# Issuing every cosine table load from ScalarE's queue in a transformer block kernel

## The chip, the cores and the metric

The kernel runs on one core of one Trainium2 chip. The metric is the device time in microseconds (us); the time before is the median of three runs. A profile of one further execution gives each engine's instructions. Engines are named as the profile names them: PE (TensorE matmuls), PEld (its weight loads), DVE (VectorE), ACT (ScalarE), POOL (GpSimd), SP (SyncE, which here only issues DMAs). A trailing q, as in SPq or ACTq, marks what an engine's sequencer does, such as issuing a DMA or waiting for a semaphore.

## What is computed

One transformer block on 2048 tokens of width 1024, all in float32:

```
h = layernorm(x)
q, k, v = h @ Wq, h @ Wk, h @ Wv           # 16 heads of 64
q, k = rotary(q), rotary(k)                # t * cos + swap_pairs(t) * sin
a = softmax(causal(q k^T) / 8) v
x = x + layernorm(a @ Wo)
f = (silu(h2 @ Wg^T) * (h2 @ Wu^T)) @ Wd^T  # h2 = layernorm(x); weights are 4-bit codes times scales
out = x + layernorm(f)
```

The change concerns the rotary step: the tables of cosines and sines, by position and feature, lie in HBM (`cos_sin`, 128 x 2 x 2048) and are loaded in pieces of 512 positions.

## The kernel before

Float32 products are made as three reduced-precision ones: each operand is split into a high part (a cast on ACT, L120) and the rest (a subtraction on DVE, L121), and `mm3` (L112 to L114) issues three matmuls. The work goes through these stages.

- **Ramp**, about 0 to 190 us. `make_x` normalizes the rows, transposes and splits them; `prep_w` loads the q, k and v weights of a feature block m of 128 columns (`wf`, L179) and splits them (L186 on ACT, L190 or L194 for the rest). `both` then calls `qkv(m, c, ..., ramp=True)` for m = 0 and 1 and the four position blocks c: eight groups.
- **Attention**, about 190 to 1320 us. For pair = 0 to 6, two heads are attended (`scores` from L262, `weighted` from L313), and beside them, between their matmuls, run the groups `qkv(m, c)` of the blocks m = 2 to 7: 24 groups that call `qkv` without `ramp`. Each of these loads its transposed rows again (`xc`, L222, four loads). For the first group of a block the three `wf` loads come ahead. The last pair's attention reaches to about 1480 us.
- **Output projection** and second layer norm, to about 1660 us, then the feed-forward part with its code lookup, to the end.

One group `qkv(m, c)` runs as follows. It takes a slot for the table `tab` and loads 512 KB into it (L232). For q and then k: 24 matmuls into a PSUM bank, a copy to `t1` by ACT (L251), a shuffle by DVE (L253), the product with the cosines by DVE (L254), that with the sines by POOL (L255), their sum by POOL (L256), a split into `hl`, and a store of 512 KB to `qs` or `ks` in HBM (L259). For v: a copy, four transposes, a split into `vo` and a store to `vs` (L249). The heads of block m read `q`, `k` and `v` back from there (L342, L335, L336).

`tab`, `vo`, both `hl` and the three `wf` all take their place from one set of four slots of 8 KB per partition, tagged "f4". A slot is free for a new tile when all that reads the old one is done: for `hl` and `vo` that is the landing of their store.

Nearly all DMAs are issued by SP, in the order of its own instruction list (`load = nc.sync.dma_start`). The only exception before is the eight table loads of the ramp, which ACT issues. An engine's instruction list, ACT's with its DMA issues included, is worked through in order; an instruction that must wait holds back all behind it.

No order is written out by hand, except a few "pace" edges that tie some matmuls of a group to matmuls of the attention. The program is built with `tile.TileContext(nc, schedule_with_timeline_sim=True)`: a planner runs the program on its own model of durations, and the order in which instructions go out there becomes the fixed order of each engine. The semaphore waits keep the result right when the chip's durations differ from the planned ones. So a change in one instruction's queue can shift the order of others behind it in all engines' lists.

Of the kernel before, what the change touches and what calls it, by code (L numbers as in the profile page):

```python
# [57 lines left out]
def block_kernel(ctx, tc, x, wq, wk, wv, wo, gu_codes, gu_scales, d_codes, d_scales, cos_sin, out):  # L58
    nc = tc.nc
    V, A, G, T = nc.vector, nc.scalar, nc.gpsimd, nc.tensor  # L60
    load = nc.sync.dma_start
# [12 lines left out]
    def slot(tag, shape, dtype, name):  # L74
        assert int(np.prod(shape[1:])) * 4 <= SLOTS[tag][1] * 1024, (tag, shape)
        return sb.tile(shape, dtype, tag=tag, name=name, bufs=SLOTS[tag][0])

    def bank(tag, name="bk"):
        return ps.tile([P, 512], F32, tag=tag, name=name, bufs=BANKS[tag])
# [22 lines left out]
    def f32(ap):  # L102
        return ap.bitcast(F32)
# [6 lines left out]
    def mm3(o, w, xx, first, last):  # L110

        r = T.matmul(o, lhsT=w[:, 0], rhs=xx[:, 0], start=first, stop=False)  # L112
        T.matmul(o, lhsT=w[:, 0], rhs=xx[:, 1], start=False, stop=False)  # L113
        T.matmul(o, lhsT=w[:, 1], rhs=xx[:, 0], start=False, stop=last)  # L114
        return r
# [3 lines left out]
    def split(hi, lo, src):  # L119
        high[:] = [A.copy(hi, src)]  # L120
        return V.tensor_tensor(lo, src, f32(hi), ALU.subtract)  # L121
# [107 lines left out]
    def qkv(m, c, ws, xs, ramp=False, pace=None):  # L229
        cs = slice(c * 512, (c + 1) * 512)  # L230
        tab = slot("f4", [P, 2, 512], F32, "tab")
        (A.dma_start if ramp else load)(tab, cos_sin[:, :, cs])  # L232
        for n, w in enumerate(ws):
            o = bank("S" if ramp and n != 1 else "F", "qkv")
            for k in range(KE):
                mm = mm3(o, w[k], xs[k // 2][:, :, k % 2, :], k == 0, k == KE - 1)
                if k == 0 and pace:
                    pace(mm, n)
            t1 = slot("t2", [P, 512], F32, "t1")
            if n == 2:  # L240
                A.copy(t1, o)
                pv = bank("F", "pv").rearrange("p (t n) -> p t n", t=4)
                for t in range(4):
                    T.transpose(pv[:, t, :], t1[:, t * P : (t + 1) * P], ident)
                vo = slot("f4", [P, 4, 2, 2, D], FR, "vo")
                src = pv.rearrange("p t (a d) -> p t a d", a=2)
                for a in range(2):
                    split(vo[:, :, a, 0, :], vo[:, :, a, 1, :], src[:, :, a, :])
                load(vs[m][cs].rearrange("(t p) a n -> p t (a n)", p=P), f32(vo.rearrange("p t a l d -> p t (a l d)")))  # L249
            else:  # L250
                A.copy(t1, o)  # L251
                sh = slot("t2", [P, 512], F32, "sh")
                V.stream_shuffle(sh, t1, [i ^ 1 for i in range(32)])  # L253
                V.tensor_tensor(t1, t1, tab[:, 0, :], ALU.mult)  # L254
                G.tensor_tensor(sh, sh, tab[:, 1, :], ALU.mult)  # L255
                G.tensor_tensor(t1, t1, sh, ALU.add)  # L256
                hl = slot("f4", [P, 2, 512], FR, "hl")
                split(hl[:, 0, :], hl[:, 1, :], t1)
                load((qs, ks)[n][m][:, :, cs], f32(hl))  # L259
# [96 lines left out]
    def both(*steps):  # L356
        for m, c in steps:
            qkv(m, c, first[m], xs[c], ramp=True)
# [25 lines left out]
    def group(m, c, xs=None, pace=None):  # L384
        if m not in ws:
            ws[m] = prep_qkv(m)
        qkv(m, c, ws[m], xs or load_x(c), pace=pace)

    for pair in range(KE - 1):
# [27 lines left out]
        for i, (m, c) in enumerate(now):  # L417

            def pace(mm, n):
                want = PACE * (3 * i + n) / (3 * len(now)) * anchors[-1][0]  # L420
                after(mm, next(a for a in anchors if a[0] >= want)[1])
# [418 lines left out]
```

## Time and profile before

| what | value |
|---|---|
| median of three runs | 3014.03 us (3012.47 to 3019.24) |
| profiled execution, its time | 3014.01 us |
| profiled execution, span of its instructions | 3012.1 us |
| busy: PE, DVE, ACT, POOL | 97%, 68%, 56%, 32% of the span |
| mean granted TensorE clock | 0.991 |
| DMA queue q1 (issued by SP) | 529.10 MB |
| DMA queue q10 (issued by ACT) | 4.19 MB, 2176 packets |
| `tab` loads | 24 from SP, 8 from ACT, 512 KB each |

The page of a profile lists busy time by engine, then the span in 40 equal slices (about 75 us each) with the busy tenths of each engine. A group row names the line, the engine, the operation and its tiles as out<-in, then the busy time and the idle time before it with what ended it. A wait row reads "who <- whom: us in total, times, longest". A timeline row gives start, duration, engine, line and, in brackets, the idle time just before and what ended it.

### The profile page before, as it was taken

How to read it: one execution, taken by the hardware profiler on the slowest of the kernel's cores; microseconds unless marked ns; L12 is line 12 of the kernel's file. 1: busy time of each engine (PE TensorE's matmuls, PEld its weight loads, DVE VectorE, ACT ScalarE, POOL GpSimd, SP SyncE). 2: the span in 40 equal slices, each digit the busy share in tenths (PEclk: the TensorE clock that was granted, in tenths of full speed). 3: DMA queues.
4: the chain of work that ended last, by engine and by line, in shares of the span. 5: the costliest groups of instructions: out<-in, count | busy, mean ns of one | idle time of the engine just before them, and what ended most of it. 6: DMA issues, size and time to landing. Idle time of an engine off the chain costs nothing.

```text
span 3012.1 us, 42532 instructions
## 1 busy us (share of the span) xinstructions
PE 2917.0 (97%) x14168; PEld 2409.7 (80%) x14168; DVE 2035.8 (68%) x4171; ACT 1698.4 (56%) x3569; POOL 953.0 (32%) x1055
## 2 busy tenths in 40 slices
PE   7989999999998999999999999999999999999998
PEld 6868888787887787777788788888888887888887
DVE  6567778886777778777665767776666677444347
ACT  4256667776666667667555655655555566333234
POOL 4344344443434343445322121222211223100034
PEclk9999999999999999999999999999999999999999
DMA  8787665757556468463456444444334444744446
GB/s 287 277 249 233 214 222 177 222 161 220 172 195 182 146 202 260 137 210 105 123 187 213 130 134 143 151 133 140 131 119 140 138 153 146 254 141 148 150 144 234
DMA packets 271740, 536.01 MB, mean 178 GB/s; under 512 B 22944, under 2 KB 113056, under 8 KB 255648
## 3 DMA queue, kind: packets, MB, share of 16 engines
q1 hardware_dynamic: 269344, 529.10, 54.6%
q10 hardware_dynamic: 2176, 4.19, 0.4%
q8 instruction: 112, 1.84, 0.3%
q14 instruction: 108, 0.88, 0.1%
HBM read 371.98 MB, written 161.22 MB: 177 GB/s over the span
## 4 chain that ended last, share of the span: by engine, by line
PE 79%; DMA 10%; DVE 4%; ACT 2%; POOL 2%; issue 1%; SPq 1%; POOLq 0%; ACTq 0%; DVEq 0%
PE bk L112 14%; PE bk L114 14%; PE bk L113 14%; PE pt L320 6%; PE qkv L112 4%; PE qkv L113 4%; PE qkv L114 4%; PE o L325 3%; PE o L324 3%; PE s L278 3%; PE s L280 3%; DMA wf<-in_wq 3%; PE pj L469 2%; PE pj L471 2%; PE pj L470 2%
## 5 line engine op out<-in xcount | busy, mean ns | idle before, releaser
L310 POOL TENSOR_SCALAR prob<-prob,rc 128x512 f32<-128x512 f32 (+3 forms) x640 | 405.4, 659 | 436.4 <-DVE rc L305 219.6
L112 PE MATMUL bk<-x,wt 128*128 128x512 f32 x1376 | 534.0, 390 | 2.7 <-ACT wt L120 1.8
L113 PE MATMUL bk<-x,wt 128*128 128x512 f32 x1376 | 535.2, 389 | 0.0
L114 PE MATMUL bk<-x,wt 128*128 128x512 f32 x1376 | 535.1, 389 | 0.0
L288 ACT ACTIVATE prob<-s,mxs 128x512 f32<-128x512 f32 (+3 forms) x640 | 402.6, 632 | 147.8 <-DVE mxs L286 90.6
L121 DVE TENSOR_TENSOR pw<-pt,pw 128x512 fp32r<-128x512 f32 (+3 forms) x640 | 378.4, 602 | 119.7 <-ACT pw L120 118.0
L534 ACT ACTIVATE ln<-cs,bias 128x512 f32<-128x512 f32 x520 | 360.0, 716 | 109.2 <-DVE m L541 25.4
L120 ACT CAST pw<-pt 128x512 fp32r<-128x512 f32 (+3 forms) x640 | 324.1, 527 | 171.6 <-PE pt L320 140.6
L320 PE MATMUL pt<-ident,prob 128*128 128x128 f32 x2176 | 345.5, 275 | 6.8 <-DVE pw L121 5.5
L320 PEld LDWEIGHTS pt<-ident,prob 128*128 128x128 f32 x2176 | 267.6, 141 | 61.7 <-issue 7.2
L112 PEld LDWEIGHTS bk<-x,wt 128*128 128x128 f32 x1376 | 258.2, 188 | 57.5 <-ACT wt L120 2.6
L286 DVE TENSOR_REDUCE mxs<-s 128x1 f32<-128x512 f32 x384 | 260.9, 681 | 60.0 <-PE s L280 59.1
L114 PEld LDWEIGHTS bk<-x,wt 128*128 128x128 f32 x1376 | 258.3, 188 | 53.8
L113 PEld LDWEIGHTS bk<-x,wt 128*128 128x128 f32 x1376 | 258.3, 188 | 53.5
L278 PE MATMUL s<-k,q 128*128 128x512 f32 (+3 forms) x640 | 265.7, 416 | 25.1 <-ACT prob L288 22.4
L325 PE MATMUL o<-pw,v 128*128 128x512 f32 (+3 forms) x640 | 247.3, 388 | 9.5 <-DVE pw L121 9.0
L324 PE MATMUL o<-pw,v 128*128 128x512 f32 (+3 forms) x640 | 244.3, 382 | 9.8 <-ACT pw L120 7.9
L112 PE MATMUL qkv<-xc,w 128*128 128x512 f32 x576 | 231.8, 402 | 10.3 <-ACT w L186 6.3
L113 PE MATMUL bk<-bt,at 128*128 128x512 f32 x616 | 239.6, 389 | 0.0
L114 PE MATMUL bk<-bt,at 128*128 128x512 f32 x616 | 238.8, 389 | 0.0
L112 PE MATMUL bk<-bt,at 128*128 128x512 f32 x616 | 238.7, 389 | 0.0
L280 PE MATMUL s<-k,q 128*128 128x512 f32 (+3 forms) x640 | 236.6, 372 | 0.0
(150 smaller groups left out, 5513.8 us busy)
## 6 DMA issues: line engine op xcount, KB each, us to landing
xc<-xd SPq DMA_DIRECT2D x96, 1024.0 KB, 9.3
q<-qs SPq DMA_DIRECT2D x128, 256.0 KB, 7.2
ast<-S SPq DMA_DIRECT2D x44, 512.0 KB, 3.9
cs<-in_gu_scales SPq DMA_DIRECT2D x172, 128.0 KB, 3.2
cs<-in_gu_codes SPq DMA_DIRECT2D x86, 256.0 KB, 3.0
A<-in SPq DMA_DIRECT2D x66, 256.0 KB, 2.0
S<-in SPq DMA_DIRECT2D x66, 256.0 KB, 3.2
ast<-A SPq DMA_DIRECT2D x33, 512.0 KB, 4.5
```

Of the source, the lines that this page charges most:

```text
L112: r = T.matmul(o, lhsT=w[:, 0], rhs=xx[:, 0], start=first, stop=False)
L113: T.matmul(o, lhsT=w[:, 0], rhs=xx[:, 1], start=False, stop=False)
L114: T.matmul(o, lhsT=w[:, 1], rhs=xx[:, 0], start=False, stop=last)
L121: return V.tensor_tensor(lo, src, f32(hi), ALU.subtract)
L278: mm = T.matmul(s, lhsT=q[:, 0, j * P : (j + 1) * P], rhs=k[:, b:e], start=True, stop=False)
L280: T.matmul(s, lhsT=q[:, 1, j * P : (j + 1) * P], rhs=k[:, b:e], start=False, stop=True)
L288: A.activation(prob[i][:, j, : e - b], s, AF.Exp, bias=mx, scale=sign, accum_out=sums[:, j % BATCH, i : i + 1])
L310: G.tensor_scalar(p, p, rc[:, jj % BATCH, i : i + 1], 0.0, ALU.mult, ALU.add)
L320: T.transpose(pt[:, j * P : (j + 1) * P], prob[kb // 4][:, j, kb % 4 * P : (kb % 4 + 1) * P], ident)
L324: T.matmul(o[:, cs], lhsT=v[:, kb, :], rhs=pw[:, 0, cs], start=kb == 0, stop=False)
L325: T.matmul(o[:, cs], lhsT=v[:, kb, :], rhs=pw[:, 1, cs], start=False, stop=kb == nk - 1)
L534: A.activation(ln, c8, AF.Prelu, bias=bias_of[ab], scale=ab[0], alpha=ab[2])
```

## The change

The choice between the two issuing engines goes away; all 32 table loads are issued by ACT. The eight of the ramp already were, so 24 loads move from SP's list to ACT's.

```
     def qkv(m, c, ws, xs, ramp=False, pace=None):
         cs = slice(c * 512, (c + 1) * 512)
         tab = slot("f4", [P, 2, 512], F32, "tab")
-        (A.dma_start if ramp else load)(tab, cos_sin[:, :, cs])
+        A.dma_start(tab, cos_sin[:, :, cs])
         for n, w in enumerate(ws):
```

Nothing else is edited: the tile, its slot, the source and the readers stay.

More of the change, by code (lines that the diff above doesn't have):

```diff
@@ L231, in qkv @@
         tab = slot("f4", [P, 2, 512], F32, "tab")
-        (A.dma_start if ramp else load)(tab, cos_sin[:, :, cs])
+        A.dma_start(tab, cos_sin[:, :, cs])
         for n, w in enumerate(ws):
```

## The prediction, made before the changed kernel ran

> **What bounds the kernel now.** I first read the busy shares by engine on the page, then a table of windows by stage, then what PE waited for inside attention, where the 24 moved loads lie (203.2 to 1305.7 us).
>
> ```profile
> PE 2917.0 (97%) x14168; PEld 2409.7 (80%) x14168; DVE 2035.8 (68%) x4171; ACT 1698.4 (56%) x3569; POOL 953.0 (32%) x1055
> ```
>
> ```profile
> 190.00:1320.00 1130.00, 1087.76 (x5868) 900.03 (x5869) 856.02 (x2197) 760.99 (x2014) 480.28 (x657) 0.99 0.63 198
> ...
> 1720.00:2520.00 800.00, 800.00 (x3531) 662.44 (x3530) 555.05 (x816) 450.80 (x705) 170.07 (x111) 1.00 0.42 136
> ```
>
> The columns of the second view are window, length, busy time of PE, PEld, DVE, ACT and POOL, granted clock, DMA share and GB/s. PE is the bound. In attention it idles 1130.0 - 1087.8 = 42.2 us; in most of the feed-forward part it never idles. ACT is busy 761 of 1130 us in attention (67%), so it has room on average, but PE's waits there end mostly with ACT:
>
> ```profile
> PE s L278 <- ACT prob L288: 17.9, 26, 2.2
> PE qkv L112 <- ACT w L186: 6.3, 3, 2.8
> PE o L325 <- DVE pw L121: 5.1, 16, 0.7
> PE o L324 <- ACT pw L120: 3.9, 3, 2.9
> PE qkv L112 <- DMA xc<-xd: 3.2, 3, 1.8
> ```
>
> ACT rows hold 17.9 + 6.3 + 3.9 = 28.1 of the 42.2 us. The score banks wait for ACT's exp, so time taken from ACT at such a moment is taken from PE. SP's queue, from which the change takes work, shows here only through loads: `xc` 3.2 us, and one `q` load 1.0 us (PE s L278).
>
> **What is removed from SP.** 24 issues at a median of 0.60 us, 14.4 us, and what those issues and their waits held:
>
> ```profile
> L232 SPq DMA_DIRECT2D tab<-in_cos_sin x24: 575/600/4478, 203.2 to 1305.7; - x24
> L232 ACTq DMA_DIRECT2D tab<-in_cos_sin x8: 547/548/624, 27.5 to 169.9; - x8
> ```
>
> The longest SP issue is the first moved load, 4.48 us at 203.2. Does an earlier table help anybody? The readers' waits say no: of those 24 loads only one was awaited (POOL, 6.4 us, at 212 us); the other waits for the table, 45.8 us of POOL and 18.6 us of DVE, belong to the ramp's eight, which do not change. What stands behind the tables in SP's list are stores of `vo`, `hl` and `ol` and loads of `k`, `q`, `v`. The only PE wait that ended with one of these loads is the 1.0 us, and `xc` goes out ahead of the table of its group. So I take **-1.0 us** (bounds: 0, and the 10.5 us of the faster rival below).
>
> The Trainium skill speaks against a gain too: "DMA: Bandwidth & Descriptors", section "Issuing engines are not separate DMA queues", says that DMAs from several engines run on the same 16 DMA engines, and that spreading them saves only the issuing sequencer's time. This trace agrees in part: four `q` loads held SP 9.97 us from 165.85, and inside that time, at 169.88, ACT's table issue took 0.55 us. Saved sequencer time can thus be more than 0.60 us per load, but by the rule alone, with SP not the bound, the -1.0 would fall away and the sum below would be 1.0 us higher.
>
> **What is added to ACT, first the issues.** 24 x 0.548 = 13.2 us of ACT's sequencer (upper bound, if every one delays PE; lower bound 0). In the ramp the instructions before an issue often still run while it is made, so most of it is covered. Of the eight, one left an open gap of ACT that only the issue explains, 0.35 us at 75.21; after the others ACT was running, or waited for something else. ACT was busy 66.5 of 190 us there (35%) and is 67% busy in attention, so I double the share: 24 x 2/8 x 0.35 = **+2.1 us**, with nothing off for PE's banks.
>
> **Then the waits.** On SP, a table load that must wait for its "f4" slot delays DMAs. On ACT, the exps and casts behind it wait, and behind those PE's score and transpose banks. Eighteen of the 24 come when, by the issues, last readers and store landings of the "f4" tiles in the timeline, at most two of the four slots are in use; I take 0 for these. The other six are the first group of each block (203, 361, 551, 751, 956 and 1166 us): three slots hold `wf`, the fourth the `vo` or `hl` before. SP's timeline at the second of them:
>
> ```profile
> 341.82 0.48 SPq L179 DMA_DIRECT2D wf<-in_wq  x1
> 342.72 0.38 SPq L179 DMA_DIRECT2D wf<-in_wk  x1
> 346.46 9.86 SPq L249 DMA_DIRECT2D vs<-vo  x1
> 356.41 1.25 SPq L179 DMA_DIRECT2D wf<-in_wv  x1
> ...
> 360.86 0.62 SPq L232 DMA_DIRECT2D tab<-in_cos_sin  x1
> ```
>
> Here and at 551 us SP's wait ended with the landing of a `vo` store:
>
> ```profile
> SPq L232 <- DMA vs<-vo: 4.2, 2, 2.1
> ```
>
> The nearest row on ACT itself is the ramp's sixth load, which waited for such a landing too:
>
> ```profile
> 133.47 0.37 ACT L120 CAST vo<-pv 128x256 fp32r<-128x256 f32 x1 [0.78 <-DVE vo L121]
> 136.31 0.55 ACTq L232 DMA_DIRECT2D tab<-in_cos_sin  x1
> 144.19 0.59 ACT L251 COPY t<-qkv 128x512 f32<-128x512 f32 x1 [10.35 <-PE qkv L114]
> ```
>
> ACT finished at 133.84 and could issue at 136.31: 2.47 us of a closed queue. There it cost nothing, because the next ACT instruction waited for PE until 144.1 anyway. In attention the next is usually an exp or a cast that is ready. How much of a closed ACT queue reaches PE is shown at 744 us, where ACT waited for a weight load:
>
> ```profile
> 748.55 1.15 ACT L186 ACTIVATE w<-wf 128x512 fp32r<-128x512 f32 x2 [4.43 <-DMA wf<-in_wq]
> ```
>
> ```profile
> 749.23 0.80 PE L112 MATMUL qkv<-xc,w 128*128 128x512 f32 x1 [2.80 <-ACT w L186]
> ```
>
> 4.43 us of ACT became 2.80 us of PE: filled banks absorb 1.63 us. With the ramp's wait and its issue a block costs 2.47 + 0.55 - 1.63 = 1.39 us, six of them **+8.3 us**. Bounds: 0, if the planner puts the load behind the landing; and, by SP's longest wait for a `vs<-vo` landing (a `v` load, 9.6 us), 6 x (9.6 + 0.55 - 1.63) = 51 us. I take the ramp's value because it is ACT's own queue and the same releaser, and SP's 2.1 us lies beside it.
>
> **Re-planning.** ACT's and SP's lists change from 203 us on, and the planner orders attention anew. The trace has no row for this; its spread can be bounded by PE's idle time in the seven equal windows of attention (161 or 162 us): 3.1, 2.9, 3.9, 8.5, 11.4, 4.9 and 7.5 us (length less PE's busy time). All seven like the best would be 7 x 2.9 = 20 us (22 less than now), all like the worst 80 us (38 more). I have no reason for either sign and take 0. From 1720 to 2520 us PE has no idle time, so a new order there should change nothing.
>
> **Sum.** -1.0 + 2.1 + 8.3 = +9.4 us. The profiled execution took 3014.01 us (span 3012.1 and 1.9 around it), equal to the median of the runs, 3014.03. Forecast: **3023.4 us**, 0.3% slower.
>
> **Rivals.**
>
> *All of it is hidden.* ACT idles a third of attention, and the planner may put the loads where the slots have long been free. For: eighteen of 24 show no full slots, and seven of the ramp's eight issues opened no gap. Against: 26 waits of PE on exps show that ACT's spare time is not there when it counts. Time: 3014.
>
> *Faster: SP's list is relieved.* After the `wf` loads SP's issues get long: `vs<-vo` 9.86 us at 346 as shown, the moved table itself 4.48 us at 203, and all behind stands still. If the loads that PE waited for go out sooner by their whole wait, PE saves `xc` 3.2, `q` 1.0 and, through ACT's weight casts, 6.3 us: 10.5 us, 3003.5. It decides once these loads come forward by 2.8 us, the longest of the waits. Against: these `xc` and `wf` loads stand ahead of their own group's table, so only a later group's can gain, and the bytes share the same engines (DMA share 0.63).
>
> *Heavy blocking.* The planner's slot release is far earlier than the chip's landing and ACT stands the full 9.6 us at all six: 3014 + 51 = 3065. Against: SP's waits at these places were 2.1 us.
>
> **How the numbers follow.** Forecast case 0.45, hidden 0.26, faster 0.22, heavy 0.07. Faster or slower by over 0.2% (6 us, about what a measurement of this kernel can tell from no change): faster 0.22, same 0.26, slower 0.45 + 0.07 = 0.52. The range reaches down through the faster case, with a little for the re-plan, to 3001; up by part of the re-plan's 38 us beyond the forecast, to 3046. It leaves out the heavy case and the low tail. The forecast case alone spans 3020 to 3046.
>
> **What would show it.** Moved at all: 32 ACTq issues on L232, none of SP, and q10 with 4 x 4.19 = 16.8 MB. Issues: ACTq near 0.55 us each; issues of several us would mean that ACT's queue backs up as SP's does. Waits: at the first group of each block, an ACT idle stretch ended by a store's landing, and PE idle after it. PE's idle time in 190 to 1320 near 42 + 9 = 52 us and the feed-forward part unchanged in length. If instead the weights' waits (6.3 us) and `xc` (3.2 us) vanish, the faster rival was right. If PE idles more with rows of exps and casts at other places than these six, the re-plan decided and my sum was for the wrong thing; if the DMA share or the clock (0.99) moves, none of it holds.

## The result and the profile after

| | before | after |
|---|---|---|
| median of the runs compared | 3019.24 us (3012.47 to 3020.93, 5 runs) | 3032.44 us (3030.26 to 3039.08, 5 runs) |
| profiled execution, its time | 3014.01 us | 3030.26 us |
| span of its instructions | 3012.1 us | 3028.5 us |
| PE's idle time, span less busy time | 95.1 us | 105.0 us |
| mean granted TensorE clock | 0.991 | 0.986 |

The changed kernel is slower: the ratio is 1.0059, interval [1.0044, 1.0073]. On 3014 us that is 17.8 us (13 to 22); the two profiled executions differ by 16.3 us. The two medians of the table alone are 13.2 us apart, the lower end of this. The forecast was +9.4 us. The profiled 16.4 us of span split into 9.9 us of idle PE and 6.5 us of busy PE, the same 14168 matmuls at a lower granted clock.

The page of the kernel after, busy shares and then the two large DMA queues (packets, MB, share of 16 engines):

```profile
PE 2923.5 (97%) x14168; PEld 2415.7 (80%) x14168; DVE 2034.8 (67%) x4171; ACT 1699.0 (56%) x3569; POOL 951.4 (31%) x1055
...
q1 hardware_dynamic: 262816, 516.51, 53.3%
q10 hardware_dynamic: 8704, 16.78, 1.6%
```

The windows by stage, after:

```profile
190.00:1320.00 1130.00, 1079.13 (x5807) 894.41 (x5808) 846.72 (x2181) 755.18 (x2000) 477.00 (x653) 0.98 0.62 195
1720.00:2520.00 800.00, 800.00 (x3532) 662.40 (x3531) 548.67 (x802) 444.42 (x695) 172.47 (x111) 1.00 0.41 135
```

The load moved as the change says (16.78 MB on q10, all of it table). The feed-forward part is untouched, PE busy for 800.00 of 800 us as before. In attention PE idles 1130.00 - 1079.13 = 50.9 us, up from 42.2. What PE waited for there, after:

```profile
PE s L278 <- ACT prob L288: 12.9, 21, 1.9
PE qkv L112 <- DMA xc<-xd: 6.5, 4, 3.0
PE o L324 <- DVE ol L328: 6.3, 2, 5.4
PE qkv L112 <- ACT w L186: 6.1, 4, 3.4
PE s L278 <- DVE pw L121: 4.8, 1, 4.8
...
PE s L278 <- DMA q<-qs: 2.6, 1, 2.6
...
PE s L278 <- DMA xc<-xd: 1.0, 1, 1.0
```

Three things are new against before. Loads: `xc` and `q` together held PE 4.2 us before and 6.5 + 2.6 + 1.0 = 10.1 us now. One wait of 5.4 us on an `ol` copy, which we follow below. And one of 4.8 us on `pw`, at 749.6 us. The waits for exps went down, 17.9 to 12.9 us. But the planner's order has changed as well, so none of these differences can be put down to the queue yet: new_order_sp, below, has the same order with the tables on SP.

**A closed ACT queue.** Of the 24 moved issues, 22 found ACT running, and together left 2.3 us of gaps. At two, ACT stood still. Here is the longer one, in ACT's, PE's and SP's timelines of the kernel after (start, duration, engine, line, operation, and in brackets the idle time before and what ended it):

```profile
1266.48 0.20 ACT L288 ACTIVATION_READ_ACCUMULATOR prob<-s,mxs 128x1 f32 x1
1270.79 0.55 ACTq L232 DMA_DIRECT2D tab<-in_cos_sin  x1
1271.43 0.58 ACT L327 COPY ol<-o 64x512 f32<-64x512 f32 x1 [4.75 <-DMA k<-ks]
```

```profile
1267.15 0.33 PE L280 MATMUL s<-k,q 128*128 128x384 f32 x1
1272.88 0.76 PE L324 MATMUL o<-pw,v 128*128 128x512 f32 x1 [5.40 <-DVE ol L328]
```

```profile
1261.72 1.91 SPq L335 DMA_DIRECT2D k<-ks  x2
```

ACT finished at 1266.68 and could not issue the table until 1270.79: 4.11 us. The wait ended with the landing of a `k` load of another head pair (the first of the two in the SP row, landed at 1270.71 by its record), which shares neither tile nor slot with the table. A DMA raises a semaphore when it lands. By the numbers in the traces, all DMAs of SP and ACT share eight of these (100 to 103 and 105 to 108), taken in turn, and both held table loads went out 0.08 us after the previous user of their semaphore had landed. Counting the SP issues from that `k` load (two `k`, one `q`, two `k`, two `xc`, one `wof`), the table is the ninth: exactly one turn. Behind the table stood the copy that frees the output bank, and PE idled 5.40 us. At 1315.62 the same happened for 1.80 us, ended by a `q` load, with 1.32 us of PE idle time behind it. Before the change such a wait held SP alone; now it holds ACT's copies, exps and casts.

**A lower clock behind it.** The stretch around it, first of before and then of after (window, length, busy times, granted clock, DMA share, GB/s):

```profile
1266.00:1280.00 14.00, 13.02 (x70) 10.45 (x69) 11.02 (x29) 10.29 (x26) 5.55 (x9) 1.00 0.84 297
```

```profile
1266.00:1280.00 14.00, 8.60 (x39) 6.73 (x38) 8.30 (x23) 7.55 (x21) 6.09 (x11) 0.76 1.04 332
```

In the same 14 us PE makes 39 matmuls in place of 70, and the mean clock is 0.76: from 1270.5 it was 0.5 for 6.8 us. So a pause costs its own length and then some of the matmuls behind it. (With another order the 14 us of before hold other work, too; a comparison of like with like follows with new_order_sp.)

### The profile page after: what moved, and what is told of

The parts are those of the page before. It is cut to its first block, busy times and chain, and to the rows that moved or that the text cites. A ratio compares the mean times of both kernels' runs of the same rounds, so it can differ in the third digit from the quotient of the medians.

```text
span 3028.5 us, 42542 instructions
## 1 busy us (share of the span) xinstructions
PE 2923.5 (97%) x14168; PEld 2415.7 (80%) x14168; DVE 2034.8 (67%) x4171; ACT 1699.0 (56%) x3569; POOL 951.4 (31%) x1055
## 3 DMA queue, kind: packets, MB, share of 16 engines
q10 hardware_dynamic: 8704, 16.78, 1.6%
## 4 chain that ended last, share of the span: by engine, by line
PE 79%; DMA 12%; DVE 4%; ACT 2%; POOL 2%; issue 1%; SPq 1%; POOLq 0%; ACTq 0%; DVEq 0%
PE bk L113 14%; PE bk L114 14%; PE bk L112 14%; PE pt L320 6%; PE qkv L112 4%; PE qkv L113 4%; PE qkv L114 4%; PE o L325 3%; PE o L324 3%; PE s L278 3%; PE s L280 3%; DMA xc<-xd 2%; DMA wf<-in_wq 2%; PE pj L471 2%; PE pj L469 2%; PE pj L470 2%
```

## The experiments

The question was threefold: is it the queue or the planner's new order; if the queue, is it ACT that is held or the tables' bytes that go out at another time; and which of the 24 loads matter. Ratios are to the kernel before, run on the same chip.

To change the queue and nothing else, the program is built twice. The first build's order is read off for every engine, and the second build gets ordering edges, without semaphores, between neighbours of each list; only the table loads are free. The traces of such a run and of the kernel whose order it holds have all 14168 matmuls in the same order, so they can be compared one by one. How much later a matmul starts than its counterpart is called PE's lag below.

```
+def keep_order(tc, plan, moved):
+    traced = {i.name: i for i in tc.nc.cur_bb.bb.instructions}
+    dep = mybir.DependencyInfo(mybir.DependencyClass.NoSync, mybir.DependencyReason.DATA)
+    for names in plan.values():
+        names = [n for n in names if n in traced and n not in moved]
+        for a, b in zip(names, names[1:]):
+            if traced[a].engine == traced[b].engine:
+                tc.add_manual_dep(traced[b], a, dep, reason="plan")
...
+    plan = engine_order(program(False, None))
+    nc = program(True, plan)
```

| run | order | tables issued by | ratio, interval | PE idle, us |
|---|---|---|---|---|
| before | old | SP | 1 | 95.1 |
| new_order_sp | new | SP | 1.0011 [1.0002, 1.0020] | 98.5 |
| after | new | ACT | 1.0059 [1.0044, 1.0073] | 105.0 |
| old_order_act | old | ACT | 1.0074 [1.0056, 1.0093] | 111.6 |
| but_two | old | ACT, 2 by SP | 1.0062 [1.0044, 1.0080] | 105.9 |
| act_later8 | old | ACT, later | 1.0058 [1.0041, 1.0075] | 109.4 |
| first6_act | old | ACT 6, SP 18 | 1.0008 [0.9996, 1.0019] | 93.8 |
| pool_tab | old | POOL | 1.0054 [1.0036, 1.0073] | 105.7 |
| act_tiny | old | SP, and 24 small ones by ACT | 1.0029 [1.0016, 1.0043] | 104.5 |
| pool_tiny | old | SP, and 24 small ones by POOL | 1.0016 [1.0002, 1.0030] | 99.4 |
| last2_sp | planned anew | ACT, 2 by SP | 1.0026 [1.0014, 1.0038] | 105.6 |
| last2_act | planned anew | SP, 2 by ACT | 1.0044 [1.0027, 1.0060] | 106.4 |

### Queue or order: old_order_act and new_order_sp

old_order_act holds the old order and moves the 24 loads:

```
-        (A.dma_start if ramp else load)(tab, cos_sin[:, :, cs])
+        t = (A.dma_start if ramp or on_act else load)(tab, cos_sin[:, :, cs]); tabs.extend([] if ramp else [t.ins.name])
```

> The 24 table loads are issued by ACT, but every other instruction of every engine keeps the order that it had before the change (edges between neighbours of each engine's old list; only the table loads are placed anew). Direct theory (ACT stands closed at the loads of the last two groups, 4.1 and 1.8 us in the changed kernel's profile, PE idles 5.4 and 1.3 us behind them, and the clock falls to half after the long one): about as slow as the changed kernel, ratio to before 1.003 to 1.007. Re-planning theory (the new order of attention costs the time, the queue does not): ratio 0.998 to 1.002. Hidden theory: 1.000.

new_order_sp has the same edit the other way round, the changed kernel's order with the tables on SP:

```
-    plan = engine_order(program(False, None))
-    nc = program(True, plan)
+    plan = engine_order(program(True, None))
+    nc = program(False, plan)
```

> The mirror image: the order of all engines is that of the changed kernel, held by edges, but the 24 table loads are issued by SP again. Direct theory: the two closed stretches of ACT go, ratio to before 0.999 to 1.002. Re-planning theory: as slow as the changed kernel, 1.004 to 1.007.

Measured: 1.0074 and 1.0011. The queue alone, in the old order, brings the whole loss; the new order alone costs 0.1%, about 3 us. The 4.8 us wait at 749.6 us belongs to the order: new_order_sp idles 5.33 us at the same place. So does a part of the waits for loads, as new_order_sp's rows show:

```profile
PE s L278 <- DMA q<-qs: 3.9, 1, 3.9
...
PE qkv L112 <- DMA xc<-xd: 1.9, 3, 1.4
```

These are 5.8 us, so of the 10.1 us after, the queue adds 4.3. At the `ol` copy, too, PE idled 2.78 us with the tables on SP, of the 5.40 us above. What the two closings cost shows in the lag of the kernel after against new_order_sp: it grows from 8.45 to 11.29 us across the first and to 13.18 us across the second, 2.8 and 1.9 us with the lower clock included, of 11.9 us at the end. That is one pair of profiles.

In old_order_act, too, ACT is closed twice, for 2.54 us at 1072.7 and 2.76 us at 1278.0, each time ended by an unrelated load; at the first, the issue at 1075.20 follows the landing at 1075.12 of an `xc` load that is again eight DMAs ahead.

### Which loads: first6_act, last2_sp, last2_act, but_two

first6_act moves only the first group of each block, the six at which the prediction put its waits:

```
+        t = (A.dma_start if ramp or on_act and c == 0 else load)(tab, cos_sin[:, :, cs]); tabs.extend([] if ramp else [t.ins.name])
```

Theory A, in what was expected here and below, is that ACT's closed queue costs the time; theory B, that the tables' bytes hold up loads for which PE waits.

> The old order, ACT issues only the table load of the first group of each block (six loads, at which the prediction had placed the whole cost of ACT's waits, 8.3 us); SP issues the other 18. By the prediction: ratio 1.003. By theory A or B, whose marks in the profiles lie at other groups: 0.999 to 1.002.

Measured: 1.0008 [0.9996, 1.0019], -1 to +6 us. ACT is closed at none of the six: at each it was still running when the load was issued, and so it was at these six in the changed kernel. The prediction's 8.3 us lie outside the interval.

last2_sp is the changed kernel with the last two groups (c = 2 and 3 of m = 7) back on SP; last2_act is the kernel before with only these two on ACT. The planner is free in both.

```
+        (load if m == KE - 1 and c >= 2 else A.dma_start)(tab, cos_sin[:, :, cs])
```

> As the changed kernel, but the loads of the last two groups (block 7, position blocks 2 and 3) are issued by SP; the planner is free, and its order equals that of the changed kernel until about 1150 us. Direct theory with the cost at these two: PE's waits of 5.4 and 1.3 us go, ratio to before 1.000 to 1.003. If the cost is in the 22 others or in the order up to there: 1.004 to 1.007.

```
+        (A.dma_start if ramp or m == KE - 1 and c >= 2 else load)(tab, cos_sin[:, :, cs])
```

> As the kernel before, but the loads of the last two groups alone are issued by ACT; the planner is free, and its order equals the old one until about 1150 us. Direct theory with the cost at these two: ratio 1.003 to 1.006. If the cost is in the 22 others: 0.999 to 1.002.

Measured: 1.0026 and 1.0044. Giving these two loads back takes the changed kernel from 1.0059 to 1.0026, and the intervals don't touch; ACT is then closed nowhere. Moving only these two costs 0.44%, with ACT closed for 3.32 us at 1256.6 and 2.51 us at 1305.3 and PE idle 4.61 and 2.03 us behind. The rest of the 24 may cost something, too: 1.0026 is above new_order_sp's 1.0011, but these two intervals overlap. Each of the two runs has an order of its own from about 1270 us (last2_sp) and 1260 us (last2_act) on. If that is worth what it was in new_order_sp, some 0.1% of these figures is order.

but_two asks the same of the old order, and takes away only the two groups at which ACT was closed in old_order_act:

```
+        t = (A.dma_start if ramp or on_act and (m, c) not in ((6, 2), (7, 2)) else load)(tab, cos_sin[:, :, cs]); tabs.extend([] if ramp else [t.ins.name])
```

> Old order of every engine, all of the 24 table loads on ScalarE's queue but the last two groups of the last two blocks (c = 2 of m = 6 and of m = 7), which stay with SyncE. In the kernel with all 24 on ScalarE in the old order (1.0074), the largest single steps against the kernel before fell near 705 us (3.4 us) and 1282 us (3.3 us). Theory A, that each step is a local cause with a price of its own: the group of block 7 with its 2.76 us closed ScalarE at 1281 is gone and with it 3 to 4 us, the rest stays: 1.005 to 1.0065, and no stretch of over 1.5 us at 1281. Rival, that a disturbance of the order in time anywhere is what costs, and that the last groups merely show it: the loss stays in proportion to the loads moved, 22/24 of 0.74%, 1.0068, with a closed stretch at another place.

Measured: 1.0062 [1.0044, 1.0080], the upper part of what the first theory gave and, by ratio alone, not far from the rival's 1.0068. The trace decides that point: ACT is closed at none of the 22 loads, so the closing did not turn up elsewhere. But the larger lesson is another: **a kernel in which ACT is never closed at a table load still loses 0.6%.** What it loses by shows in PE's waits of but_two:

```profile
PE qkv L112 <- DMA xc<-xd: 9.7, 4, 3.4
...
PE s L278 <- DMA q<-qs: 2.7, 1, 2.7
```

12.4 us for loads, against 4.2 before, with the same order of every engine. Not each of them is a loss: 2.79 us of idle time end at 701.25 with an `xc` load that landed 0.1 us earlier than before, and PE had only come to it sooner. Five other waits for loads (four for `xc`, one for `q`, spread over the stage) are longer than before by 1.2 to 1.8 us each, 7.0 us in all.

### Held engine or moved bytes: act_tiny, pool_tab, pool_tiny, act_later8

How can a load on another queue make SP's loads late? Compare the group at 690 us, before (SP, then PE):

```profile
692.29 0.32 SPq L222 DMA_DIRECT2D xc<-xd  x1
693.38 0.58 SPq L232 DMA_DIRECT2D tab<-in_cos_sin  x1
```

```profile
701.37 0.51 PE L112 MATMUL qkv<-xc,w 128*128 128x512 f32 x1 [0.31 <-DMA xc<-xd]
```

with old_order_act (ACT, SP, then PE):

```profile
688.26 0.55 ACTq L232 DMA_DIRECT2D tab<-in_cos_sin  x1
```

```profile
695.00 0.33 SPq L222 DMA_DIRECT2D xc<-xd  x1
```

```profile
705.07 0.80 PE L112 MATMUL qkv<-xc,w 128*128 128x512 f32 x1 [3.67 <-DMA xc<-xd]
```

In SP's list the table stood behind the group's last `xc` load, 1.1 us later. ACT isn't held by SP's list and sends its 512 KB 6.7 us ahead of that load. By the records the `xc` load then took 10.03 us to land in place of 9.04. PE needs `xc` at once, while the table is first read after the group's 24 matmuls for q; PE waits 3.67 us in place of 0.31. Only 1.0 us of the difference is the longer time to landing. SP issued the load 2.7 us later because the whole kernel ran 2.7 us late by then, while PE had caught up to 0.3 us: before, it had just lost 2.19 us and run at half clock. Nor does this loss last: PE's lag is 6.0 us at 720 us and 1.9 at 759. At 853 us the same happens, and the loss stays: the table goes 7.1 us ahead, `xc` goes out 2.1 us later than PE's lag explains and takes 10.40 us in place of 9.26, and the lag goes from 1.9 to 6.5 us.

The table goes ahead of its group's last `xc` load in only 3 of the 24 groups. It needn't go first to be in the way. The group at 300 us, before (SP):

```profile
298.25 1.83 SPq L222 DMA_DIRECT2D xc<-xd  x2
300.18 0.61 SPq L232 DMA_DIRECT2D tab<-in_cos_sin  x1
```

and with old_order_act (SP, ACT, PE):

```profile
299.80 1.84 SPq L222 DMA_DIRECT2D xc<-xd  x2
```

```profile
303.69 0.55 ACTq L232 DMA_DIRECT2D tab<-in_cos_sin  x1
```

```profile
314.08 0.50 PE L112 MATMUL qkv<-xc,w 128*128 128x512 f32 x1 [1.77 <-DMA xc<-xd]
```

Here the table goes out 2.4 us after the second `xc` load, in place of 0.4. By the records it lands 0.5 us ahead of that load, where on SP's queue it landed 1.3 us behind. The two `xc` loads take 14.24 and 14.97 us in place of 12.29 and 13.46, and PE waits 1.77 us where it had not waited.

A third effect is the turn of eight itself, in which a table on ACT stands at another place. In the group at 690 us, SP sent the last `xc` load as soon as the second of three `q` loads had landed (692.27 us). In old_order_act, with the table in the turn ahead, it had to wait for the third (694.98 us, 1.0 us after the second).

To separate the held engine from the moved bytes, act_tiny leaves the tables where they were and has ACT issue a 4 KB load, which nobody reads, at each place where old_order_act has a table:

```
+        tiny = const.tile([P, 2, 4], F32, name="tiny")
+        names = [A.dma_start(tiny, cos_sin[:, :, 4 * j : 4 * j + 4]).ins.name for j in range(len(tabs))]
+        place = dict(zip(tabs, names))
+        plan[acts] = [place.get(x, x) for x in extra[acts]]
```

> The old order on all engines, and the tables loaded by SP as before. In addition ACT issues a load of 4 KB, which nobody reads, at each of the 24 places in its list where the table load stands in old_order_act: the issues and ACT's waits are there, the 512 KB on ACT's queue are not. Theory A (ACT's closed queue and its issues cost the time): ratio to before 1.004 to 1.008. Theory B (the tables' bytes leave ACT's queue ahead of xc and q loads for which PE waits, and these land later): 1.000 to 1.003.

pool_tab has the tables issued by POOL, so that no ACT instruction stands behind them:

```
+        t = (A.dma_start if ramp else G.dma_start if on_act else load)(tab, cos_sin[:, :, cs]); tabs.extend([] if ramp else [t.ins.name])
```

> The old order on all engines, the 24 tables issued by POOL: the bytes leave neither in SP's order nor through ACT. Theory A: ratio 0.999 to 1.002, since ACT has no issue and no wait more. Theory B: the tables still run beside the xc and q loads, 1.003 to 1.007, with PE's waits for xc and q over twice the 4.2 us of before.

pool_tiny is act_tiny with `G.dma_start` for the added loads, placed in POOL's list as pool_tab has its tables.

> Old order of every engine, all tables loaded by SyncE as before, and 24 added loads of 4 KB that nobody reads, issued by GpSimd at the places at which it issues the tables in the run pool_tab. The same added loads issued by ScalarE gave 1.0029. Theory, that there ScalarE's queue, closed until an unrelated load had landed, is the cause: from GpSimd no ScalarE instruction is held, 0.9995 to 1.0008, and ScalarE has no closed stretch of over 1.5 us at a load. Rival, that any 24 further transfers with their completions shift the rest: 1.002 to 1.004 here too.

Measured: 1.0029, 1.0054 and 1.0016. Without ACT in it, the tables on another queue cost 0.54%, most of the 0.74%; ACT is closed nowhere in that run, and PE's waits for `xc` and `q` are 5.3 + 1.0 + 2.9 = 9.2 us. (Its waits for exps rose as well, from 17.9 to 21.8 us. POOL issues for itself there, and its own work moves a little, so not every bit of it need be bytes.) pool_tiny has POOL's issues without the 512 KB: its interval doesn't touch pool_tab's, and the difference is some 0.4%. POOL's DMAs have eight semaphores of their own (111 to 118), so the turn of SP and ACT has none of the 24 tables in it.

The times to landing tell the same. SP's list is the same in these runs, so the 92 `xc` loads that it issues from 195 us on can be compared one by one with before. In old_order_act 16 take over 1 us longer to land, and 4 over 1 us less; in pool_tab 24 and 8. With the 4 KB loads it is 5 and 9 (act_tiny), 5 and 5 (pool_tiny).

The held ACT alone costs up to 0.29%: in act_tiny ACT is closed for 4.56 us at a 4 KB load, and PE idles 4.97 us behind it. The added loads take places in the turn of eight, too, and that is in this figure. pool_tiny lies between its two theories. 24 more small transfers cost something even from POOL, so of act_tiny's 0.29% perhaps 0.13% is due to ACT; but the two intervals overlap, and that figure is not shown.

act_later8 keeps the old order and puts each table eight ACT instructions later than old_order_act has it:

```
+    plan = {e: shifted(names, tabs, 8) for e, names in plan.items()}
```

> As old_order_act, but each of the 24 table loads stands eight instructions (some 5 us) later in ACT's list, with all else held. Theory B: most tables fall behind the last xc load of their group again, ratio 1.001 to 1.004 against the 1.0074 of old_order_act. Theory A: ACT's waits move to other places but do not go: 1.005 to 1.009.

Measured: 1.0058, within theory A's range; theory B's 1.001 to 1.004 lies below the interval. The waits for `xc` fall from 10.6 us in old_order_act to 2.4 + 0.9, nearly before's 3.2, since no table goes out ahead of its group's `xc` any more. But `q` still holds PE 4.7 us, and ACT is closed at three other places, for 2.96, 1.79 and 2.63 us. A fixed shift moves the collision; it doesn't take it away, and bytes ahead of `xc` are not the whole of the loss. No version tried is faster than the kernel before. A table put earlier within SP's own list, which would show overtaking with no second queue in it, was not tried.

## Why the prediction was right or wrong

- **The bound** (PE; ACT's and the loads' moments count, not their averages): right. The feed-forward part unchanged: right.
- **-1.0 us for SP's relief**: wrong sign, and the largest miss. The argument looked for loads that stand behind the table in SP's list and would go sooner. It did not ask what the table's 512 KB do to the loads ahead of it once they are no longer behind them in one queue. `xc` and `q` waits of PE rose from 4.2 us before, and 5.8 in new_order_sp, to 10.1 after (9.2 in pool_tab, 12.4 in but_two). The faster rival said itself that "the bytes share the same engines", but only as a limit on the gain. The priority that SP's single list had given to `xc` is what the change removed.
- **+2.1 us for the issues**: right in size on ACT's side, 2.3 us of gaps at 22 loads, at 0.55 us each issue. That it reaches PE is not shown.
- **+8.3 us for ACT waits at the first group of each block**: wrong place and wrong cause. At those six nothing waited (first6_act, 1.0008). The "f4" slot was not what closed ACT.
- **0 for the other eighteen**: wrong. A slot was the only wait counted. The table also waits for the DMA one turn of eight ahead of it to land, and at two of the eighteen this closed ACT for 4.11 and 1.80 us. The profile of before had such waits on SP: its table load at 693.38 us went out 0.06 us after the `q` load eight DMAs ahead had landed.
- **1.63 us absorbed by filled banks**: about right as a price. By the prediction's sum (wait + 0.55 - 1.63) the two closings cost 3.0 and 0.7 us; PE's lag against new_order_sp grew by 2.8 and 1.9, the lower clock included. So ACT's waits came to some 4.7 us at two places that the prediction had put at nothing, in place of 8.3 at six.
- **0 for the new order**: right in size, +0.11% (new_order_sp).
- **The clock**: not priced. It went from 0.991 to 0.986, and busy PE time rose by 6.5 us; new_order_sp was busy for 2917.2 us, as before (2917.0), so this is not the order's. The prediction had named a moved clock as a sign that its account doesn't hold. PE's idle time in attention came out at 50.9 us where 52 were forecast; with the clock's share missing, that agreement is a coincidence of two terms that were wrong in opposite ways.
- So slower was right and 3023.4 too low, since a closed ACT was there but the bytes and the clock came on top. That the time lies inside 3001 to 3046 is in part luck: the largest term stood at the wrong places, and the largest effect was entered as a small gain. The heavy rival's shape (ACT held for several us) appeared twice, not six times. The hidden rival fails by the ratio's interval.

What stays open is how the loss splits. Parts measured alone don't add up exactly: 0.54% (tables by POOL; some 0.4% less pool_tiny's share) and 0.29% (ACT) make 0.83% (or 0.67%) where both together are 0.74%, all within the intervals; the two last groups cost 0.33 to 0.44%, and all but the two closed ones 0.62%. Taking the closings away in the old order saved 0.12% (1.0074 to 1.0062), with overlapping intervals. It is shown that the queue and not the order costs most of the time, that the tables' 512 KB on another queue are enough for some 0.4%, and that ACT's closings occur and leave PE idle. What a closing is worth rests on one pair of profiles. The share of the turn of eight was not measured by itself.

## What to carry to other kernels

A queue is also a priority list: before a load is moved off a shared queue, look at what it stood behind, and ask what its bytes do to that load if they no longer go behind it. On an engine that computes, a DMA issue is worth its 0.55 us only while none of its waits is open, so list all of them, those of the program's own completion counting too, at every place and not only where buffers are short. To tell a moved queue from a re-planned order, hold the old order and move only the queue.

## What the runs showed of the hardware

- A DMA that takes 0.55 us to issue held ACT for up to 4.56 us, even at 4 KB, until a DMA of SP that shared no tile with it had landed; the eight completion semaphores taken in turn couple SP's and ACT's queues in this program.
- The granted clock fell to 0.5 after short pauses of PE. Before: 2.19 us idle up to 697.45 and 3.4 us at 0.5 from 697.3; 1.91 us idle up to 1024.56 and 6.8 us at 0.5 from 1025.0. After: 1.25 us idle up to 860.82, with 0.67 us just ahead of it, and 3.4 us at 0.5 from 860.9. The Trainium skill, "TensorE: Matmul & The Clock Gate", "Part 1: The HAM clock gate", gives one idle window of about 3.4 us as what it takes to fall back; the rows above fell back after less, so here the measurement decides. Not every such pause did it: 2.52 us idle up to 1370.51 before left the clock at 1.0.
- The Trainium skill, "DMA: Bandwidth & Descriptors", section "Issuing engines are not separate DMA queues", says that several issuing engines only save sequencer time. In these runs the choice of engine also changed which bytes landed first (at 300 us a table load issued 2.4 us after an `xc` load landed 0.5 us ahead of it), and cost 0.54% (POOL) to 0.74% (ACT).
